# Preparing the first attention group of an adaptive-norm block: q and k written straight into the scores' rows, the preparation in source order, and maxima by half sequences

## The chip, the cores and the metric

The kernel runs on one core of a Trainium2 chip. The metric is the device time of one execution in microseconds; the time before is the median of three executions. Engines are named as in the profile: PE is TensorE's matrix products, PEld its weight loads, DVE is VectorE, ACT is ScalarE, POOL is GpSimd, SP is SyncE, whose queue issues most of the DMAs.

## What is computed

A transformer block with adaptive layer norms on x of shape (4, 1024, 256), in float32, 16 heads of 16. Shapes below are those of one of the 4 batches where nothing else is said.

```python
mod = (silu(c) @ wmod).reshape(4, 6, 1, 256)
sa, ca, ga, sb, cb, gb = six parts of mod          # ga, gb: at least 0.25 in size
h = layernorm(x) * (1 + ca) + sa
q, k, v = split(h @ qkv_w.T)                       # 16 heads of 16
att = softmax(q @ k.T / 4) @ v
x = x + ga * (att @ proj_w.T + proj_b)
h = layernorm(x) * (1 + cb) + sb
loss[n] = mean((relu(h @ W_enc[n] + b_enc[n]) @ W_dec[n] + b_dec[n] - h) ** 2)   # 8 experts
n = connected_idx[argmin(loss)]
x = x + gb * (h @ W_base + b_base + relu(h @ W_down[n] + b_down[n]) @ W_up[n] + b_up[n])
```

## The kernel before

**Scores twice.** Four heads make a group; there are 4 batches x 4 groups = 16 groups. For each, the kernel needs the maximum of every row of scores ahead of the softmax. So it makes the scores twice. First untransposed: `row_max` (L409) makes `ps` = q by k for 128 queries, 512 keys and two heads at a time (L448), and VectorE reduces it (L455). One such tile is a pair, and a group has 32. Then transposed: `step_of`'s `begin` (L534) makes `pt` = k by q, adds the rows' maxima `mt` by a second product with the constant `pick` (L542), and ScalarE takes the exponential `es` (L550). `weigh` (L502) multiplies `es` by v with a column of ones beside each column, `vaug` (L506). A group has 16 steps (2 halves of 512 queries by 8 tiles of 128 keys), each with two `pt` tiles; 256 steps in all.

**Rows of the scores.** To be exact enough in the fast 32-bit mode, q and k are each split in a rounded part and the rest. A row of 16 dimensions becomes 64 rows: q rounded, q rounded, q rest, q rest against k rounded, k rest, k rounded, k rest. `qk_chunk` (L326) makes q or k of eight heads (128 rows by 512 columns) and splits it into `qhl`/`khl`; `expand` (L393) then writes each of the four parts by its own DMA of 32 rows to every fourth partition of `q64`/`k64` (L402).

**Maxima to rows.** When a set of pairs is done, `to_row` (L414) turns the maxima by a PE transpose `pmx` (L416), copies and splits them (DVE, POOL) and sends them by `mdram` to DRAM and back to `mt` (L423, L431). The argument `apart` makes this happen once for each half of the queries; otherwise once for the group. Only the first group has it.

**Order.** PE's instructions are in source order by hand (`manual_schedule`, L82). The other engines' order is decided by a scheduler from the source order and the dependences. The preparation (L896 to L988) makes the condition `cs` (L140) from `c`, turns the weights (`turn_weights`, L153), makes the modulation (`modulation`, L160), normalises the first batch (`norm_items`, L252, through `norm_first`, L301), makes q and k of the first eight heads and spreads two groups of them, fills constants (`mt`, `pick`, `vaug`), and starts the remaining loads (`load_rest`, L199). Then 16 pairs of the first group run, and after each of them one item of the list `beside` (L959): weight turns for v, the products for v (L370), the second modulation, the gate rows (L182), the turns for proj, the biases. Then come the first maxima's `to_row`, four pairs more, and the main loop.

**Pace of the maxima.** In the main loop, `wanted(k)` (L984) says how many pairs shall be given by step k. Before: 20 at step 0, 32 at step 4, 64 at step 12, and from then each group is complete five steps ahead of its first step. Dense work beside (q and k of later heads, v, projections, the experts) is spread over the steps by streams of items.

**Buffers.** Three PSUM tiles of two banks (`big`) serve `ps`, `pt` and the experts' `pr`; two single banks (`acc`, `msc`) serve the rest and, through `spare_tile`, the preparation. `xin` has three buffers for x of later batches; `fu` (L351) has one.

Of the kernel before, what the change touches and what calls it, by code (L numbers as in the profile page):

```python
# [8 lines left out]
F32 = mybir.dt.float32  # L9
# [8 lines left out]
P = 128  # L18
# [8 lines left out]
def tile_adaln_block(  # L27
# [54 lines left out]
    ctx.enter_context(tc.manual_schedule(engines={mybir.EngineType.PE}))  # L82
# [13 lines left out]
    qn = stage.tile([P, 3 * NC, D], F32, name="qn")  # L96
    qkv_rows = qkv_w.rearrange("(o p) i -> p o i", p=P)
    nc.scalar.dma_start(qn[:, : 2 * NC, :], qkv_rows[:, : 2 * NC, :])
    wm = stage.tile([P, NC, 6 * D], F32, name="wm")
    wmod_rows = wmod.rearrange("(c p) e -> p c e", p=P)  # L100
    nc.sync.dma_start(wm[:, :, : 2 * D], wmod_rows[:, :, : 2 * D])
    for u in range(NT // 4, NT // 2):
        x_in[0, u] = load_two(0, u)
    nc.scalar.dma_start(qn[:, 2 * NC :, :], qkv_rows[:, 2 * NC :, :])
    nc.scalar.dma_start(wm[:, :, 2 * D :], wmod_rows[:, :, 2 * D :])
    pn = stage.tile([P, NC, D], F32, name="pn")
    nc.scalar.dma_start(pn, proj_w.rearrange("(o p) i -> p o i", p=P))
# [5 lines left out]
    nc.gpsimd.memset(neghalf, -0.5)  # L113

# [38 lines left out]
    def turn_weights(dst, src, o, tile):  # L153

        pt = tile([P, NC, P], f"pw_{dst.name}_{o}")
        for c in range(NC):
            nc.tensor.transpose(pt[:, c, :], src[:, o, c * P : (c + 1) * P], ident)
        nc.scalar.copy(dst[:, :, o * P : (o + 1) * P], pt)

    def modulation(first, tile):  # L160
# [13 lines left out]
        nc.vector.tensor_copy(modc[:, first], pm[:, 0])  # L174
        nc.vector.tensor_scalar_add(modc[:, first + 1], pm[:, 1], 1.0)
# [125 lines left out]
    def norm_first(b, between=()):  # L301
# [3 lines left out]
        items = [("X", alloc)]  # L305
        for half in range(NH):
            items += norm_items(
                lambda t, half=half: x_in[b, (half * TH + t) // 2][:, t % 2, :],
                lambda: hT_of[b],
                SA,  # L310
                CA,
                b,
                half,
                f"n1_{b}_{half}",
                b == 0,
            )
            if half == 0:
                items += between
        return items
# [6 lines left out]
    def qk_chunk(b, ch):  # L326
        def part(n, which, h, c, s={}):
# [17 lines left out]
            if c == NC - 1:  # L345
                hl = split[key]
                if alone:
                    nc.scalar.copy(hl[:, 0, hs], pq)
                    nc.vector.tensor_tensor(hl[:, 1, hs], pq, hl[:, 0, hs].bitcast(F32), ALU.subtract)
                    return  # L350
# [42 lines left out]
    def expand(b, g, i):  # L393

        ch, r0 = g // GC, (g % GC) * HG * HD
        for which, order in (("q", (0, 0, 1, 1)), ("k", (0, 1, 0, 1))):
            hl = split[which, b, ch]
            t = wa.tile([P, S], F32R, tag=f"{which}64{i}", name=f"{which}64_{b}_{g}_{i}", bufs=3)
            r = slice(r0 + 2 * i * HD, r0 + (2 * i + 2) * HD)
            for n, part in sorted(enumerate(order), key=lambda x: x[1]):  # L400
                queue = nc.scalar if alone and which == "k" and g == 0 else nc.sync
                queue.dma_start(t[n::4, :].bitcast(F32), hl[r, part, :].bitcast(F32))  # L402
            duos[which, b, g, i] = t

# [4 lines left out]
    def row_max(b, g, apart=False):  # L409
# [30 lines left out]
        for halves in [[hq] for hq in range(NH)] if apart else [list(range(NH))]:  # L440
            pairs = [(i, hq, t, h) for i in range(2) for hq in halves for t in range(TH) for h in range(NH)]
            for i, hq, t, h in pairs:
# [452 lines left out]

    cs = condition()  # L896
    for o in range(2 * NC):
        turn_weights(wqkv, qn, o, big_tile)
    modulation(SA, big_tile)
    all_of(Stream(norm_first(0)))  # L900
    all_of(Stream(qk_chunk(0, 0)))
    for g in range(2):
        for i in range(2):
            expand(0, g, i)
    mean_w = cst.tile([P, P], F32, name="mean_w")
    nc.gpsimd.memset(mean_w, 1.0 / (S * D))
    iota_i = cst.tile([P, NE], I32, name="iota_i")
    nc.gpsimd.iota(iota_i, pattern=[[1, NE]], base=0, channel_multiplier=0)
    iota_e = cst.tile([P, NE], F32, name="iota_e")
    nc.vector.tensor_copy(iota_e, iota_i)  # L910
    part_i = cst.tile([P, 1], I32, name="part_i")
    nc.gpsimd.iota(part_i, pattern=[[0, 1]], base=0, channel_multiplier=1)
    part_f = cst.tile([P, 1], F32, name="part_f")
    nc.vector.tensor_copy(part_f, part_i)

    mt = []
    for n in range(2):
        t = cst.tile([P, S], F32R, name=f"mt{n}")  # L920
        nc.gpsimd.memset(t.bitcast(F32), 0.0)
        mt.append(t)
    picks = []
    for i in range(2):
        t = cst.tile([P, 1], F32, name=f"row{i}")
        nc.vector.tensor_tensor(t, ident[:, i : i + 1], ident[:, 2 + i : 3 + i], ALU.add)
        for r in (DUO + i, DUO + 2 + i):
            nc.vector.tensor_tensor(t, t, ident[:, r : r + 1], ALU.add)
        pick = cst.tile([P, P], F32R, name=f"pick{i}")
        nc.vector.tensor_copy(pick, t.to_broadcast([P, P]))  # L930
        picks.append(pick)

    NV = NG + 1
    vaug = []
    for n in range(NV):
        t = cst.tile([P, NT, HG, STRIP], F32, name=f"vaug{n}")
        nc.gpsimd.memset(t, 1.0)
        vaug.append(t)
    mpad = []
    for n in range(2):  # L940
        t = cst.tile([P, P], F32, name=f"mpad{n}")
        nc.gpsimd.memset(t, 0.0)
        mpad.append(t)

# [12 lines left out]


    beside = [lambda o=o: turn_weights(wqkv, qn, o, spare_tile) for o in range(2 * NC, 3 * NC)]  # L959
    beside += [lambda item=item: [f() for f in item[2]] for item in v_all(0)]  # L960
    beside += [lambda: modulation(SB, spare_tile), lambda: gate_rows(spare_tile)]
# [244 lines left out]
```

## Time and profile before

| | us |
|---|---|
| median of 3 executions | 1191.78 (1190.69 to 1195.03) |
| the profiled execution | 1194.91, its span 1193.1 |
| first pair of scores (`ps`) | at 42.47 |
| transpose of the first maxima (`pmx`) | at 72.24 |
| first exponential (`es`) | at 80.00 |
| one maximum of a pair, DVE | 1.22 |
| one exponential, ACT | 1.02 |

The mean granted clock of TensorE is 0.978 of full. Times in the profile are microseconds from the start of the span unless marked ns. A group of instructions is told by its line, its engine and `out<-in` by the program's names, then how many there were. Of each wait, the profile names the engine or DMA that ended it. The time at which an engine is idle costs nothing unless the engine bounds the time. The granted clock (PEclk) is a share of the full TensorE clock. A product in full 32-bit shows as two records, one in the fast mode as one.

### The profile page before, as it was taken

To read this page: it belongs to the slowest core of one execution; us is meant where nothing else is said; L and a number is where in the kernel's file an instruction comes from. 1 tells how busy PE (TensorE), PEld (TensorE's weight loads), DVE (VectorE), ACT (ScalarE), POOL (GpSimd) and SP (SyncE) were. 2 spreads that over 40 slices of the span, in tenths; PEclk is the share of its full clock that TensorE was granted. 3 is DMA by queue.
4 is the path that set the end of the run, shared out by engine and by line. 5 is a ranking of instruction groups with operands and counts; after the bars stand their busy time and mean duration, and the time that the engine had idled before them with its cause. 6 is when DMAs were issued, how large, how long until landed. Compare 5 with 4: busy or idle time off the path is not lost.

```text
span 1193.1 us, 16436 instructions
## 1 busy us (share of the span) xinstructions
PE 1077.8 (90%) x6324; PEld 476.5 (40%) x6324; DVE 791.9 (66%) x975; ACT 692.3 (58%) x928; POOL 254.8 (21%) x271
## 2 busy tenths in 40 slices
PE   4768889999999889999999889999999889899995
PEld 3423333434444333345444333345444333344443
DVE  4477977777687666767678666676778777701264
ACT  2114466665666677654556667654655676647662
POOL 3155000200314002240224201140222200042003
PEclk9869999999999999999999999999999999999998
DMA  6522130122121201113131200204040300011001
GB/s 203 142 81 55 41 77 18 50 69 54 44 60 36 61 15 48 54 43 82 38 110 27 56 15 24 64 27 103 17 131 8 76 1 18 15 58 53 18 1 47
DMA packets 42582, 63.92 MB, mean 54 GB/s; under 512 B 13052, under 2 KB 28436, under 8 KB 42504
## 3 DMA queue, kind: packets, MB, share of 16 engines
q1 hardware_dynamic: 40000, 58.41, 18.2%
q10 hardware_dynamic: 1736, 3.15, 0.8%
q0 software_dynamic: 768, 1.31, 0.5%
q8 instruction: 50, 0.82, 0.3%
q14 instruction: 28, 0.23, 0.1%
HBM read 19.39 MB, written 5.19 MB: 21 GB/s over the span
## 4 chain that ended last, share of the span: by engine, by line
PE 69%; ACT 11%; DVE 10%; DMA 4%; issue 4%; POOL 2%; SPq 0%; ACTq 0%; DVEq 0%; POOLq 0%
PE pt L542 18%; PE pv L506 18%; PE ps L448 10%; ACT es L550 6%; DVE mx L455 5%; PE ph L626 4%; PE pr L647 3%; PE pq L338 3%; PE pvp L370 3%; ACT df L655 3%; DVE df L650 3%; PE ppj L591 2%; PE pf L761 2%; PE pk L338 2%; PE ptn_n L284 2%
## 5 line engine op out<-in xcount | busy, mean ns | idle before, releaser
L455 DVE TENSOR_REDUCE mx<-ps 128x2 f32<-128x1024 f32 x512 | 611.8, 1220 | 191.9 <-PE ps L448 188.2
L550 ACT ACTIVATE es<-pt 128x1024 f32<-128x1024 f32 x512 | 510.8, 1022 | 296.2 <-PE pt L542 289.5
L506 PE MATMUL pv<-es,vaug 128*32 128x512 f32 x2048 | 274.6, 607 | 0.1
L448 PE MATMUL ps<-k,q 64*128 64x512 f32 x1024 | 236.4, 461 | 35.0 <-ACT es L550 10.4
L542 PE MATMUL pt<-q,k 64*128 64x512 f32 x1024 | 239.0, 451 | 21.8 <-ACT es L550 10.7
L542 PE MATMUL pt<-mt,pick 64*128 64x512 f32 x1024 | 209.4, 393 | 4.6 <-DMA mt<-mdram 4.6
L448 PEld LDWEIGHTS ps<-k,q 64*128 64x128 f32 x1024 | 98.3, 186 | 201.4 <-issue 92.5
L542 PEld LDWEIGHTS pt<-q,k 64*128 64x128 f32 x1024 | 99.3, 184 | 170.7 <-DVE mx L455 96.8
L655 ACT ACTIVATE df<-df,fbias 128x512 f32<-128x512 f32 x128 | 91.1, 713 | 55.0 <-DVE df L650 55.0
L542 PEld LDWEIGHTS pt<-mt,pick 64*128 64x128 f32 x1024 | 100.4, 186 | 15.6 <-DMA mt<-mdram 5.8
L650 DVE TENSOR_TENSOR df<-pr,h2T 128x1024 f32<-128x1024 f32 x64 | 77.4, 1222 | 42.5 <-PE pr L647 20.7
L506 PEld LDWEIGHTS pv<-es,vaug 128*32 128x32 f32 x2048 | 40.5, 108 | 100.1 <-issue 90.8
L647 PE MATMUL pr<-he,wdec 64*128 64x512 f32 x256 | 64.3, 614 | 6.3 <-ACT es L550 6.2
L484 POOL TENSOR_TENSOR aT<-aT,su 128x512 f32<-128x512 f32 x14 | 17.8, 1273 | 238.9 <-DMA su<-rdram 189.5
L626 PE MATMUL ph<-h2T,wenc 128*128 128x512 f32 x128 | 63.6, 623 | 0.0
L781 DVE TENSOR_TENSOR x<-pf,x 128x512 f32<-128x512 f32 x16 | 10.8, 687 | 54.3 <-PE pf L772 22.1
L353 POOL CAST qhl<-fu_q 128x512 fp32r<-128x512 f32 x14 | 8.5, 610 | 178.4 <-ACT fu_q L352 175.9
L267 POOL TENSOR_TENSOR rstd_n<-ve_n,neghalf 128x4 f32<-128x4 f32 x16 | 16.8, 1048 | 102.2 <-DVE ve_n L265 96.4
L761 PE MATMUL pf<-wbg,h2T 128*128 128x256 f32 x128 | 37.4, 425 | 0.0
L647 PEld LDWEIGHTS pr<-he,wdec 64*128 64x128 f32 x256 | 21.6, 185 | 37.3 <-ACT es L550 13.2
L284 PE MATMUL ptn_n<-ident,xh_n 128*128 128x128 f32 x128 | 23.2, 311 | 14.0 <-ACT h2T L285 6.6
L626 PEld LDWEIGHTS ph<-h2T,wenc 128*128 128x128 f32 x128 | 22.3, 192 | 33.0 <-issue 31.8
(134 smaller groups left out, 755.8 us busy)
## 6 DMA issues: line engine op xcount, KB each, us to landing
q<-qhl SPq DMA_DIRECT2D x128, 128.0 KB
k<-khl SPq DMA_DIRECT2D x120, 128.0 KB
xin<-in_L_attn_x_dram SPq DMA_DIRECT2D x16, 256.0 KB
x<-in_L_attn_x_dram SPq DMA_DIRECT2D x8, 512.0 KB
aT<-ou SPq DMA_DIRECT2D x32, 128.0 KB
out_dram<-x SPq DMA_DIRECT2D x16, 256.0 KB
su<-rdram SPq DMA_DIRECT2D x14, 256.0 KB
wm<-in_L_wmod_dram ACTq DMA_DIRECT2D x1, 1024.0 KB
```

The costliest lines, as they stand in the source:

```text
L284: nc.tensor.transpose(pt[:, t, :], s["xh"][:, t, c * P : (c + 1) * P], ident)
L338: nc.tensor.matmul(pq, wqkv[:, c, n * D + ch * P : n * D + (ch + 1) * P], hT[:, c, hs], start=(c == 0), stop=(c == NC - 1),)
L448: nc.tensor.matmul(ps[:, a, :], q[r, t0 : t0 + P], k[r, h * HALF : (h + 1) * HALF], start=True, stop=True,)
L455: nc.vector.tensor_reduce(mx[:, h, hq, i::2, t], ps, AX.X, ALU.max, negate=True)
L506: nc.tensor.matmul(acc[h][j * STRIP : (j + 1) * STRIP, :], va[:, kt, j, :], es[j // 2][:, j % 2, :], start=(kt == 0), stop=(kt == NT - 1),)
L542: nc.tensor.matmul(pt[:, a, :], k[r, kt * P : (kt + 1) * P] if first else picks[i][r, :], q[r, hs] if first else mt[n % 2][r, hs], start=f ...
L550: nc.scalar.activation(e, pt, AF.Exp, scale=SCALE)
L626: nc.tensor.matmul(s["ph"], wenc[:, c, 2 * pr : 2 * pr + 2, :].rearrange("p n h -> p (n h)"), s["h2T"][:, c, hs], start=(c == 0), stop=(c ...
L647: nc.tensor.matmul(two[:, i, :], wdec[r, pr, c * P : (c + 1) * P], he[r, :], start=True, stop=True)
L650: nc.vector.tensor_tensor(df, two, h2T[:, c, hs].unsqueeze(1).to_broadcast([P, 2, HALF]), ALU.subtract)
L655: nc.scalar.activation(df[:, i, :], df[:, i, :], AF.Square, bias=bdec_of(e, c), accum_out=s["acc"][:, e, c, h : h + 1],)
L761: nc.tensor.matmul(po[u][:, t, :], s["h2T"][:, c, t0 : t0 + P], s["wbg"][:, c, :], start=(c == 0), stop=False,)
```

## The change

1. **Order.** From the start of the preparation until the main loop, ACT, DVE, POOL and SP also keep the source order; the source is rearranged for it. The constants, zeros and ones come first, then the statistics of the first half of x, `cs`, the normalised first half, the weights, the second half's statistics, the modulation. Of `vaug` only the columns of ones are filled, not all. A tile `warm` and three products of it (`keep_on`) are added.
2. **Loads.** x of the first batch is first in SP's queue, the q and k weights and the first part of `wmod` in ACT's; the v weights, the rest of `wmod` and the proj weights follow in SP's. The v weights lie in a buffer of `xin`.
3. **First group.** For its heads, q and k are not spread by DMA. `turn_weights` also writes the turned weights with every column four times (`wide`, in two `xin` buffers). A product with `wide` then gives 128 rows, each dimension four times, for two heads (`widened`): ScalarE rounds it into `fu`, and VectorE writes `fu` times `less` plus the product, where `less` is -1 in the rows that hold a rest and 0 in the others. There are four such products for the first half of the sequence, ahead of the first scores, and two more (k's second half) beside them. q's second half comes by DMA from the ordinary split (`second_half`).
4. **Beside.** The four q and k products of the first eight heads, which came before the scores, are now items of `beside`, and their split goes over GpSimd as it does later in the kernel. The turns of the remaining q and k weights come at its end.
5. **expand** uses two DMAs of 64 rows for q and two for k in place of four and four of 32 rows; all on SP.
6. **Maxima.** In all four groups of the first batch the maxima go to `mt` by halves of the queries, and the order of pairs within a half is keys' half, head pair, tile. `wanted` now asks 20 at step 0, 32 at step 3, then runs evenly to 160 at step 59, the first batch's end; later batches as before.
7. The modulation's two results are copied by ScalarE, not VectorE.

```diff
-    ctx.enter_context(tc.manual_schedule(engines={mybir.EngineType.PE}))
+    ctx.enter_context(tc.manual_schedule(engines={ET.PE}))
+    begin_order = ctx.enter_context(ExitStack())
+    begin_order.enter_context(tc.manual_schedule(engines={ET.Activation, ET.DVE, ET.Pool, ET.SP}))
...
-    nc.sync.dma_start(wm[:, :, : 2 * D], wmod_rows[:, :, : 2 * D])
+    nc.scalar.dma_start(wm[:, :, : 2 * D], wmod_rows[:, :, : 2 * D])
...
+    vn = xin.tile([P, NC, D], F32, tag="xin", name="vn")
+    wide = {w: xin.tile([P, NC, D], F32, tag="xin", name=f"wide_{w}") for w in "qk"}
+    nc.sync.dma_start(vn, qkv_rows[:, 2 * NC :, :])
+    nc.sync.dma_start(wm[:, :, 2 * D :], wmod_rows[:, :, 2 * D :])
...
-        nc.gpsimd.memset(t, 1.0)
+        nc.gpsimd.memset(t[:, :, :, 1::2], 1.0)
...
+        if wide is not None:
+            for c in range(NC):
+                nc.scalar.copy(
+                    wide[:, c, :].rearrange("p (j n) -> p j n", n=4),
+                    pt[:, c, : HG * HD].unsqueeze(2).to_broadcast([P, HG * HD, 4]),
+                )
...
-                if alone:
-                    nc.scalar.copy(hl[:, 0, hs], pq)
-                    nc.vector.tensor_tensor(hl[:, 1, hs], pq, hl[:, 0, hs].bitcast(F32), ALU.subtract)
-                    return
...
-            for n, part in sorted(enumerate(order), key=lambda x: x[1]):
-                queue = nc.scalar if alone and which == "k" and g == 0 else nc.sync
-                queue.dma_start(t[n::4, :].bitcast(F32), hl[r, part, :].bitcast(F32))
+            for n in range(2):
+                rows = hl[:, n : n + 1, :].to_broadcast([2 * HD, 2, S]) if which == "k" else hl
+                nc.sync.dma_start(t[n::2].bitcast(F32), rows)
...
+    def widened(which, i, h):
+        hs = slice(h * HALF, (h + 1) * HALF)
+        key = (which, 0, 0, i)
+        if key not in duos:
+            duos[key] = wa.tile([P, S], F32R, tag=f"{which}64{i}", name=f"{which}64_0_0_{i}", bufs=3)
+        pq = spare_tile([P, HALF], f"pw{which}_{i}_{h}")
+        for c in range(NC):
+            nc.tensor.matmul(
+                pq,
+                wide[which][:, c, i * P : (i + 1) * P],
+                hT_of[0][:, c, hs],
+                start=(c == 0),
+                stop=(c == NC - 1),
+            )
+        fu = wa.tile([P, HALF], F32, tag="fu", name=f"fu_{which}_{i}_{h}", bufs=1)
+        nc.scalar.copy(fu.bitcast(F32R), pq)
+        nc.vector.scalar_tensor_tensor(duos[key][:, hs], fu, less[which], pq, ALU.mult, ALU.add)
+
+    def second_half(i):
+        hl = split["q", 0, 0][2 * i * HD : (2 * i + 2) * HD, :, HALF:].bitcast(F32)
+        for n in range(2):
+            nc.sync.dma_start(duos["q", 0, 0, i][n::2, HALF:].bitcast(F32), hl)
...
+            if apart:
+                pairs = [(i, hq, t, h) for hq in halves for h in range(NH) for i in range(2) for t in range(TH)]
...
+    first, second = [Stream(items) for items in norm_first(0)]
+    all_of(first, most=TH + 1)
     cs = condition()
-    for o in range(2 * NC):
-        turn_weights(wqkv, qn, o, big_tile)
+    keep_on(1)
+    keep_on(2)
+    all_of(first, most=TH)
+    for o, w in ((0, "q"), (NC, "k")):
+        turn_weights(wqkv, qn, o, big_tile, wide=wide[w])
+    all_of(second, most=TH + 1)
     modulation(SA, big_tile)
...
+    widened("k", 0, 0)
+    widened("q", 0, 0)
+    widened("k", 1, 0)
+    all_of(second)
+    widened("q", 1, 0)
...
+    beside = [lambda i=i: widened("k", i, 1) for i in range(2)]
+    beside += [lambda item=item: [f() for f in item[2]] for item in qk_chunk(0, 0) if item[0] == "D"]
...
-            yield from row_max(b, g)
+            yield from row_max(b, g, apart=b == 0)
...
-        ends = [(0, FIRST + 4), (4, PAIRS), (STEPS - 4, 2 * PAIRS)] + [
-            (first_step[bg] - LEAD, PAIRS * (n + 3)) for n, bg in enumerate(groups[2:])
+        ends = [(0, FIRST + 4), (3, PAIRS)] + [
+            (first_step[bg] - LEAD, PAIRS * (n + 1)) for n, bg in enumerate(groups) if bg[0]
         ]
```

## What was predicted

> **What bounds the kernel now.** I read the totals first, then the engines by stretches of 20 us, then the chain of waits for the first 140 us, because everything in the diff but one line lies ahead of the main loop.
>
> From part 1 of the page:
>
> ```profile
> PE 1077.8 (90%) x6324; PEld 476.5 (40%) x6324; DVE 791.9 (66%) x975; ACT 692.3 (58%) x928; POOL 254.8 (21%) x271
> ```
>
> TensorE is the bound of the whole: 115.3 us of the 1193.1 us span are all that it idles. So a change here can pay only by idle time of TensorE or by time at a low clock. Where these lie is told by the stretches (start:end, length, PE busy, PEld, DVE, ACT, POOL, then granted clock, DMA share, GB/s):
>
> ```profile
> 0.00:20.00 20.00, 2.65 (x11) 1.69 (x11) 9.83 (x33) 2.95 (x6) 8.61 (x18) 1.00 0.89 272
> 20.00:40.00 20.00, 14.53 (x48) 9.35 (x48) 6.91 (x29) 5.45 (x8) 9.04 (x15) 0.95 0.41 97
> 40.00:60.00 20.00, 17.53 (x71) 11.21 (x72) 9.77 (x10) 3.88 (x18) 0.00 (x0) 0.76 0.53 144
> 60.00:80.00 20.00, 11.80 (x43) 5.27 (x42) 16.14 (x24) 1.49 (x4) 8.48 (x8) 0.67 0.27 81
> 80.00:100.00 20.00, 16.49 (x78) 6.04 (x74) 13.53 (x16) 8.19 (x9) 19.62 (x18) 0.77 0.19 57
> 100.00:120.00 20.00, 17.65 (x101) 7.03 (x101) 16.77 (x18) 8.93 (x10) 4.94 (x7) 1.00 0.26 65
> 120.00:140.00 20.00, 16.14 (x92) 6.54 (x92) 18.29 (x17) 9.30 (x10) 1.88 (x2) 1.00 0.23 59
> 220.00:240.00 20.00, 20.00 (x120) 8.47 (x120) 13.38 (x12) 11.89 (x14) 5.22 (x6) 1.00 0.25 66
> ```
>
> The first four rows hold 46.5 us of PE work in 80 us: 33.5 us idle, and the clock falls to 0.67. The next three idle 9.7 us more. From 140 to 220 us PE works 73.28 of 80 us, from 220 to 340 us 117.79 of 120: there is little left to win. The first exponential starts at 80.0 us, and that is the point from which I measure the two halves of the sum. The chain of waits up to there (start, length, what):
>
> ```profile
> 9.74 10.19 issue
> 19.92 3.55 PE pm L167 x16
> 27.28 3.87 PE pq L338 x8
> 38.46 4.00 DMA q<-qhl
> 42.47 0.80 PE ps L448 x2
> 62.68 9.15 DVE mx L455 x8
> 72.24 0.45 PE pmx L416
> 83.28 2.50 DMA xin<-in_L_attn_x_dram
> ```
>
> Three holes are seen: PE waits 10.2 us for the condition `cs` (VectorE makes it only at 19.7 us, behind work whose `xin` landed late), 7.9 us for the spreading DMAs of q and k, and from 62.7 us on it runs at the pace of VectorE's maxima (8 in 9.15 us, with the clock at 0.5 to 0.7).
>
> **The change, part by part.**
>
> *Front to the first score.* The order of the built program is now fixed for all engines. VectorE has 12 small operations on `ident`, then `iota_e`, which waits for GpSimd. GpSimd first fills two `mt` (0.94 and 1.04 us) and five `vaug`, 1.02 us each at 1024 elements (5.12 us for five). They now write 512 elements at a stride of two. No row shows a strided fill: 0.5 us each if it goes by elements, 1.0 if by the span; I take 0.5, since 128 elements cost 0.2 and 1024 1.02. So `iota_e` at about 6.3 us (8.9 at the other end). VectorE's small operations took 0.8 to 1.1 us where they lay beside those fills, so I add 1 us. Then the first half's statistics, as in the row from 3.69 to 5.84 us: 2.1; and three operations for `cs`, 0.5: `cs` at about 10 us, not 19.8. The weights `wm` are 512 KB in the second queue behind `qn`; at the 272 GB/s of the first row, the 2 MB of x, q/k weights and `wm` are there by 8 to 10 us. pm: 3.55 us as at 19.9, or 1.95 as at 56.4; I take 3, and with modc end at 13.5. The first half's transposes and their two activations (23.47 to 26.09 us before): 2.6, to 16.1. Then in PE's order three widened products (four records of 0.48, so 1.93 each by the row of pq), two transpose groups (1.9), the fourth product: 4 x 1.93 + 1.9 = 9.6, and 0.8 for handing tiles to ScalarE and VectorE and back. **First score at about 26.5 us, not 42.5**; 24.5 to 30 with the ends above. Two warm-up products before the weights and the extra copies of `wide` on ScalarE (4 x 0.4) lie in the wait for `cs`; were that gone they would cost 3 us.
>
> At this place a rule speaks against the sum. The Trainium skill (TensorE: Matmul & The Clock Gate, Parts 1 and 4) says that full clock needs some 3.4 us of sustained activity and that transposes do not count as busy. By it, pm and eight transposes leave the array cold, and the first two products cost 3.9 instead of 1.93 each: 30.4 us. But the row of before has just pm and sixteen transposes from 19.92 to 27.28, and then pq at 3.85 for 8 records, full speed. I go by the row.
>
> *The stage of the first maxima.* It holds more PE work than before, for two widened products and the four of the ordinary q and k have come into it. Sixteen pairs of scores x 0.5 = 8; six products x 1.93 = 11.6; v's two weight turns 1.0; gate rows 2.5 (3.2 at the low clock before); four v products x 1.95 = 7.8; pm 1.9; the proj and remaining q/k turns and biases, 2.4: 35.2. To this 1.8 for waits: the single buffer `fu` now goes through GpSimd (cast 0.61 + difference 1.27), which also makes four normalised tiles of the next batch (1.21 each) in between; that holds ScalarE in order, hence v's weight copies. 26.5 + 37 = 63.5 for the transpose of the maxima, not 72.2. VectorE's sixteen maxima (19.6) no longer trail: they are hidden under 37 us of PE work. From that transpose to the first exponential it took 7.8 us (72.24 to 80.0), four steps of which stay as they are: **first exponential at about 71.5, 8.5 us earlier**. Bounds 67.5 and 78.
>
> *The main loop, to step 59.* Before, `wanted` asks 4 pairs a step up to step 12, then 2.1 and 2. Now it asks 4 a step for three steps and 128 pairs over 56 steps, 2.3 a step. The first 60 us after 80 hold 40 maxima and 23 exponentials, 5.2 us a step; from 140 to 220 us 52 and 47, 3.4 us a step. The pairs are not removed: TensorE gets each one's 0.45 us later. So the worth is idle and cold time. Idle 9.7 in 60 us (16%) should come to the 8.4% of the next 80 us, whose load of maxima, 2.2 a step, is nearest: 4.6 gained. Low clock from 80 to 100 (0.77): 3 gained, if PE enters warm; it again has some 5 us of idle before the first exponential, so 2. Against it: three more max transposes, 1 us. And VectorE's queue: after the fourth maximum of the second half come the statistics of the next batches' x. Of these the one that reads `xin_1` waits for a load that waits for GpSimd to have centred the tiles before it, and GpSimd now has the gated projection weights (1.29), the gated bias (0.73) and two additions (1.23 each) ahead of that. Queued behind the waiting statistics are two maxima, and behind them both score tiles and so TensorE. Before, VectorE idled 1.8 us here; I get 4.5 (load at 81.0, maxima done at 76.5): minus 2.7, between 0 and -7. Loop: +2.9, between -4 and +10.
>
> *Rest.* q and k spread by half as many DMAs of twice the bytes, on SP only: the 0.6 us that each issue takes is halved. In their new order, SP's loads of the next x wait for PE's last use of `wide` (27 and 32 us), behind them lie the second halves of q (39, when GpSimd has split it), group 1's rows (49) and the gate rows (56); the first of these is asked for at 64, group 1 at 80. GpSimd waits for `conn_i` behind 5 MB of loads, 20 us at 272 GB/s, and has nothing due before 34. So all of it has slack; in the whole loop PE waited 4.6 us for `mt` and for spread q or k only once, at 42 us. I take 0; were the slack gone, a late spread would cost its 4 us once per group. From batch 1 the plan is as before: 0.
>
> Sum: 1194.9 (span 1193.1 and 1.8 around it) - 8.5 - 2.9 = 1183.5. That execution stands 3.1 above the median of 1191.8, so against the median I say **1180.4**.
>
> **The rivals.**
> *A, as summed* (0.50): 1174 to 1185.
> *B, the loop takes it back* (0.20): the pairs put off return in steps 12 to 59, where PE idles only 6.7 us from 140 to 220, and VectorE's stall is at its long end. For it: TensorE is the bound, and 2.3 pairs a step are more than what the 140-to-220 stretch carries. Against: 9.7 us of idle just before. 1191.8 - 8.5 + 4 = 1187.
> *C, both halves at their good ends* (0.17): first exponential at 67.5 and +7 in the loop: 1191.8 - 12.5 - 7 = 1172, or a few less.
> *D, slower by a low clock* (0.13): between 12 and 63.5 us PE has 50 us of work at full clock, with eight widened products (15.4 us) that it did not have. The clock was 0.76 and 0.67 from 40 to 80 us of before. At 0.85 throughout, 9 us are lost and the 8.5 are gone; at 0.7, 21: 1191.8 - 11.4 + 21 = 1201. Against: those low stretches had PE waiting; between 50 and 58 us, dense, it shows 1.00.
>
> **The numbers.** Differences below 0.5%, 6 us, are about what a measurement of this kernel cannot tell from none. Faster by more (below 1185.8): nearly all of A, C, a third of B: 0.70. Within: 0.18. Slower (over 1197.8): most of D: 0.12. The range, 1167 to 1193, leaves out D and C's far end; A's own is 1174 to 1185.
>
> **What would show it.** In the changed profile: first score near 26.5, max transpose near 63.5, first exponential near 71.5 us; no wait of scores for q's spreading; the clock at 0.9 or more from 20 to 60 us; about 32 maxima in the first 11 steps; VectorE idle near 77 to 81 us on `xin`; from step 59 the same pace as now. It is wrong if `cs` comes after 14 us, if the clock from 15 to 60 us is under 0.85, or if PE idles over 16 us in the 140 us after the first exponential.

## The result, and the profile after

The changed kernel takes 1199.31 us (median of 6 executions, 1198.30 to 1200.87), the kernel before, run beside it, 1193.4 (1189.54 to 1199.05, 6 executions): a ratio of 1.0046, 95% interval 1.0026 to 1.0067. Predicted were 1180.4 us, with 1167 to 1193 as the range. The change costs about 6 us where 11 us of gain were expected. The profiled execution took 1198.3 us with a span of 1196.5; before it was 1194.91 and 1193.1.

Part 1 of the page of the changed kernel, as before:

```profile
PE 1094.1 (91%) x6357; PEld 482.2 (40%) x6357; DVE 797.7 (67%) x980; ACT 697.3 (58%) x942; POOL 261.6 (22%) x285
```

TensorE idles 102.4 us of the span instead of 115.3, and is still slower: it has 16.3 us more busy time, with only 33 more records. Part of that is work at half clock. The stretches (columns as before: start:end, length, PE, PEld, DVE, ACT, POOL, granted clock, DMA share, GB/s):

```profile
0.00:20.00 20.00, 16.44 (x45) 8.98 (x46) 14.15 (x44) 5.66 (x14) 7.63 (x21) 0.83 0.87 264
20.00:40.00 20.00, 18.98 (x56) 7.40 (x54) 14.01 (x21) 6.08 (x10) 7.00 (x13) 1.00 0.12 31
40.00:60.00 20.00, 17.80 (x87) 11.38 (x85) 11.11 (x10) 6.54 (x27) 15.04 (x12) 0.97 0.74 166
60.00:80.00 20.00, 11.19 (x39) 4.83 (x41) 11.93 (x23) 3.23 (x5) 13.25 (x13) 0.50 0.33 95
80.00:100.00 20.00, 18.34 (x93) 7.44 (x97) 15.05 (x19) 8.23 (x9) 10.18 (x12) 0.85 0.09 27
220.00:240.00 20.00, 18.93 (x127) 7.49 (x123) 15.08 (x14) 12.79 (x15) 4.49 (x6) 1.00 0.31 69
```

The first 60 us are what they were meant to be: from 20 to 60 us TensorE is busy for 36.8 of 40 us, at a granted clock of 0.98. The hole is now one, from 60 to 80 us: 11.19 us of work at a clock of 0.50. The chain of waits up to there (start, length, what):

```profile
10.06 2.84 PE pm L227 x16
14.79 3.39 PE pwk L472 x4
18.18 1.72 PE pwq L472 x4
25.46 0.65 PE ps L534 x3
75.42 2.67 DMA xin<-in_L_attn_x_dram
```

PE no longer waits for spread rows of q, and the first exponential starts at 68.25 us instead of 80.00. So where did that lead go? Each step's first exponential (`es`, L636, before L550) was read off both traces. This is how much earlier (minus) or later it stands than before, with four of the experiments told of below:

| step | before at, us | changed | e1 | e2 | e6 | e13 |
|---|---|---|---|---|---|---|
| 0 | 80.0 | -11.8 | -10.5 | +1.5 | -10.4 | -14.0 |
| 4 | 103.3 | -6.0 | -3.8 | +1.0 | -4.0 | -16.2 |
| 12 | 143.9 | -17.6 | -15.4 | +1.0 | -15.6 | -26.7 |
| 60 | 309.2 | -6.9 | -4.7 | +1.0 | -4.8 | -14.7 |
| 128 | 598.7 | -6.7 | -4.7 | +2.6 | -4.7 | -15.0 |
| 144 | 657.9 | -1.0 | -5.4 | +7.7 | -5.4 | -15.4 |
| 192 | 874.0 | -0.1 | -5.5 | +8.6 | -5.5 | -14.2 |
| 208 | 934.2 | +4.4 | -6.3 | +14.5 | -6.4 | -15.2 |
| 255 | 1123.8 | +4.1 | -6.5 | +12.7 | -3.1 | -13.3 |

Four things are in the column "changed". The front gains 11.8. The first four steps give 5.8 of it back. Steps 4 to 12 gain another 11.6, and steps 12 to 60 take 10.7 back. And in three short stretches, at about 602, 683 and 885 us, 11 us are lost for good (5.7, 0.9 and 4.5), in batches whose plan was said to be as before.

VectorE at the loop's start shows the first loss (the timeline; in brackets the idle time before the instruction and what ended it):

```profile
78.12 0.43 DVE L320 BATCH_NORM_STATS2 bs_n<-xin 128x6 f32<-128x256 f32 x1 [7.02 <-DMA xin<-in_L_attn_x_dram]
78.46 2.34 DVE L541 TENSOR_REDUCE mx<-ps 128x2 f32<-128x1024 f32 x2
```

The statistics are those of batch 2's x (counted from 0), put by the scheduler some 60 steps ahead of their place in the source. The two maxima behind them wait too, and with them both score tiles.

The second kind of loss is at 602 us. First SP's queue of the changed kernel, the time of each issue, then VectorE:

```profile
596.79 0.57 SPq L461 DMA_DIRECT2D k<-khl  x1
597.46 0.53 SPq L605 DMA_DIRECT2D aT<-ou  x1
598.04 1.25 SPq L615 DMA_DIRECT2D sdram<-ou  x1
599.38 0.60 SPq L461 DMA_DIRECT2D k<-khl  x1
600.03 0.59 SPq L461 DMA_DIRECT2D q<-qhl  x1
600.98 0.77 SPq L554 DMA_DIRECT2D rs<-sdram  x1
```

```profile
597.99 1.23 DVE L541 TENSOR_REDUCE mx<-ps 128x2 f32<-128x1024 f32 x1 [0.21 <-PE ps L534]
604.59 0.35 DVE L557 RECIPROCAL rs<-rs 128x32 f32<-128x32 f32 x1 [5.38 <-DMA rs<-sdram]
604.86 2.29 DVE L541 TENSOR_REDUCE mx<-ps 128x2 f32<-128x1024 f32 x2
```

`sdram` takes the softmax sums out to DRAM (8 KB), `rs` brings them back as 128x32 (16 KB), and VectorE's reciprocal stands in its queue among the maxima. It waits 5.38 us. Before, the same place looks like this, with two spreads of k of 128 KB between the first two lines:

```profile
601.72 0.56 SPq L529 DMA_DIRECT2D sdram<-ou  x1
605.20 0.53 SPq L468 DMA_DIRECT2D rs<-sdram  x1
607.36 0.35 DVE L471 RECIPROCAL rs<-rs 128x32 f32<-128x32 f32 x1 [1.33 <-DMA rs<-sdram]
```

The wait was 1.33 us. Over the whole kernel, VectorE's idle time in front of the 14 reciprocals is 17.0 us in seven waits, before 5.3 in six. TensorE, which gets no score tile while VectorE stands, also falls to half clock for 6.8 us from 604.8.

### The profile page after: what moved, and what is told of

It is laid out like the page before. It is cut to its first block, busy times and chain, and to the rows that moved or that the text cites. A ratio compares the mean times of both kernels' runs of the same rounds, so it can differ in the third digit from the quotient of the medians.

```text
span 1196.5 us, 16380 instructions
## 1 busy us (share of the span) xinstructions
PE 1094.1 (91%) x6357; PEld 482.2 (40%) x6357; DVE 797.7 (67%) x980; ACT 697.3 (58%) x942; POOL 261.6 (22%) x285
## 4 chain that ended last, share of the span: by engine, by line
PE 70%; ACT 11%; DVE 8%; DMA 4%; issue 4%; POOL 2%; SPq 0%; DVEq 0%; ACTq 0%; POOLq 0%
PE pt L628 18%; PE pv L592 18%; PE ps L534 10%; ACT es L636 6%; PE ph L712 4%; PE pr L733 3%; PE pq L400 3%; ACT df L741 3%; PE pvp L428 3%; DVE df L736 2%; PE ppj L677 2%; DVE mx L541 2%; PE pk L400 2%; PE pf L847 2%; PE ptn_n L344 1%
## 5 line engine op out<-in xcount | busy, mean ns | idle before, releaser
L636 ACT ACTIVATE es<-pt 128x1024 f32<-128x1024 f32 x512 | 510.9, 1022 | 308.3 <-PE pt L628 299.5
L534 PEld LDWEIGHTS ps<-k,q 64*128 64x128 f32 x1024 | 99.1, 188 | 192.8 <-issue 76.5
L628 PEld LDWEIGHTS pt<-mt,pick 64*128 64x128 f32 x1024 | 101.7, 188 | 15.6 <-DMA mt<-mdram 6.2
L504 POOL CAST mrow<-mfull 32x128 fp32r<-32x128 f32 x20 | 5.6, 281 | 199.2 <-DVE mfull L502 199.2
L867 DVE TENSOR_TENSOR x<-pf,x 128x512 f32<-128x512 f32 x16 | 10.8, 687 | 54.2 <-PE pf L858 22.1
L327 POOL TENSOR_TENSOR rstd_n<-ve_n,neghalf 128x4 f32<-128x4 f32 x16 | 16.6, 1034 | 88.4 <-DVE ve_n L325 84.6
L344 PE MATMUL ptn_n<-ident,xh_n 128*128 128x128 f32 x128 | 21.9, 296 | 15.2 <-ACT h2T L345 6.5
```

Source lines behind the costliest of these rows:

```text
L534: nc.tensor.matmul(ps[:, a, :], q[r, t0 : t0 + P], k[r, h * HALF : (h + 1) * HALF], start=True, stop=True,)
L628: nc.tensor.matmul(pt[:, a, :], k[r, kt * P : (kt + 1) * P] if first else picks[i][r, :], q[r, hs] if first else mt[n % 2][r, hs], start=f ...
L636: nc.scalar.activation(e, pt, AF.Exp, scale=SCALE)
```

## The experiments

Theory S: the two bigger spreading DMAs make `rs` late, and VectorE's reciprocal passes that on. Its first rival, L: TensorE is the bound, the loop takes any lead back, and the places are accidental. Each time of before was measured beside the kernel that it stands with.

**e1: four spreads in the loop.** `expand` of before for the main loop, that of the change in the preparation.

```diff
+            if not alone:
+                for n, part in sorted(enumerate(order), key=lambda x: x[1]):
+                    nc.sync.dma_start(t[n::4, :].bitcast(F32), hl[r, part, :].bitcast(F32))
```

> The changed kernel, but q and k of the main loop are again spread by four DMAs of 32 rows each instead of two of 64; the preparation keeps its two. Theory S (the small load of the sums, rs, comes late behind the bigger spreading DMAs in SP's queue, VectorE's reciprocal waits 5.4 us for it in order, and TensorE waits for the maxima behind that): the lead of 6.9 us that the changed kernel still has at step 128 is kept to the end, the waits for rs at about 602 and 885 us fall to about 1.5 us, time about 1188 (11 less than the changed kernel's 1199, 5 less than before). Rival L (TensorE bounds the loop and takes the lead back in any case, the three losses of 5.7, 1.0 and 4.5 us only happen to stand at those places): the losses reappear at other places and the time is 1197 or more.

Measured: 1187.39 us, before 1193.37; ratio 0.9954 (0.9941 to 0.9966). The lead of 4.7 us at step 128 is kept to the end. At the same place SP and VectorE show:

```profile
596.98 0.56 SPq L620 DMA_DIRECT2D sdram<-ou  x1
598.69 1.13 SPq L466 DMA_DIRECT2D k<-khl  x2
599.92 0.54 SPq L559 DMA_DIRECT2D rs<-sdram  x1
```

```profile
602.05 0.35 DVE L562 RECIPROCAL rs<-rs 128x32 f32<-128x32 f32 x1 [0.91 <-DMA rs<-sdram]
```

This kernel stands 2.0 us later at this place. Allowing for that, `sdram` is issued 3.1 us earlier than in the changed kernel, and `rs` lands 2.1 us after its issue instead of 3.6. The first spread of k, on which SP stood until GpSimd had cast `khl` at 596.76, now comes behind `sdram`, not ahead of it. VectorE's order is the same: the reciprocal follows the 286th maximum in both.

**e2: only the two spreads.** The other direction: before, with two DMAs of 64 rows in the loop.

```diff
+            if not alone:
+                for n in range(2):
+                    rows = hl[r].bitcast(F32)
+                    if which == "k":
+                        rows = rows[:, n : n + 1, :].to_broadcast([2 * HD, 2, S])
+                    nc.sync.dma_start(t[n::2].bitcast(F32), rows)
```

> The kernel before, with only this part of the change: q and k of the main loop are spread by two DMAs of 64 rows each. Theory S: SP's queue then has the same order as in the changed kernel (sums out, two DMAs of 256 KB, rs, two more), VectorE waits some 5.4 us for rs at two or three places, and the time is some 11 us above before, about 1204. Rival L: half as many issues of twice the bytes make no difference, within 2 us of before.

Measured: 1205.75 us, ratio 1.0108 (1.0079 to 1.0137). This part alone costs 12 us, and the waits for `rs` sum to 19.0 us. S holds both ways so far as the spreads go, and L falls: e1 kept the whole lead that it had at step 128. What passes the lateness on is left to e6.

**e3: the old pace of maxima**, `apart` for the first group alone.

```diff
-            yield from row_max(b, g, apart=b == 0)
+            yield from row_max(b, g)
...
-        ends = [(0, FIRST + 4), (3, PAIRS)] + [
-            (first_step[bg] - LEAD, PAIRS * (n + 1)) for n, bg in enumerate(groups) if bg[0]
+        ends = [(0, FIRST + 4), (4, PAIRS), (STEPS - 4, 2 * PAIRS)] + [
+            (first_step[bg] - LEAD, PAIRS * (n + 3)) for n, bg in enumerate(groups[2:])
```

> The changed kernel with the pace of maxima of before (64 pairs at step 12, each group complete five steps ahead) and the maxima by halves only for the first group. Theory P (the pairs put off are a loan: from step 12 to 59 they are paid back one for one): the lead over before at step 12 is only about 8 us, not 17.6, at step 60 it is 7 as in the changed kernel, and the time is within 3 us of the changed kernel's. Rival (the even pace itself costs TensorE idle time, since VectorE is then asked for 2.3 maxima in each step of 12 to 59): the lead at step 60 stays near 11 us and the time falls by 4 or more.

Measured: 1199.82 us, ratio 1.0052 (1.0037 to 1.0068), as the changed kernel. The lead is 6.7 us at step 12 and 6.7 at step 60. So the even pace is a loan: 11 us lent by step 12, all paid back by step 60, and worth nothing.

**e4: source order kept for eight steps more**, on ACT, DVE, POOL and SP.

```diff
-    begin_order.close()
...
     for k0 in range(0, len(order) * NT, 2):
+        if k0 == 8:
+            begin_order.close()
```

> The changed kernel, but the source order of ACT, DVE, POOL and SP is kept for eight steps more, into the main loop, so that the statistics of a later batch's x can't be put ahead of the loop's maxima in VectorE's queue. If VectorE's wait of 7.0 us for xin at 71 to 78 us is real loss: it is gone, the first exponential is some 4 us earlier, the lead at step 12 is larger, and the time is about 5 us less, 1194. If it lies beside the wait for the maxima's way through DRAM to mt anyway: the first exponential stays at 68 and the time within 2 us of the changed kernel's.

Measured: 1204.88 us, ratio 1.0096 (1.0070 to 1.0122): a miss. The wait of 7.0 us is gone, and the lead at step 8 is 19.7 us instead of 11.8. But the statistics only come later, and wait for `xin` there: 2.6 us at 97.5, 5.5 at 116.6, 3.5 at 139.4 us. At step 60 the lead is 0.6. The wait is a real loss, and it moves with the statistics.

**e5: `rs` issued by GpSimd**, in the changed kernel.

```diff
-        nc.sync.dma_start(rs, sdram[n].rearrange("j (a c) -> (j a) c", c=few[0]))
+        nc.gpsimd.dma_start(rs, sdram[n].rearrange("j (a c) -> (j a) c", c=few[0]))
```

> The changed kernel with its two big spreading DMAs, but the one small load rs (16 KB, 14 of them) is issued by GpSimd's queue instead of SP's; nothing else is moved by it but one maximum past one reciprocal. Theory S (the loss of 12 us is the lateness of rs in SP's queue, passed on by VectorE's in-order reciprocal): VectorE's idle time in front of the reciprocals falls from 17.0 us to 5 or less, the waits at about 602 and 885 us go, and the time is about 1188. Rival T (the bigger transfers cost the same time on other ways: they hold the DMA engines, or the other small transfers of SP's queue come late too): 1195 or more.

Measured: 1206.35 us, ratio 1.0097 (1.0073 to 1.0120): worse than the changed kernel, and a miss for S, which had 1188. VectorE's waits before reciprocals rise to 28.3 us. At the place of 602 us `sdram` is still issued behind a spread of k and held for 1.22 us. GpSimd stands idle in front of nine of its 14 issues of `rs` until `sdram<-ou` has landed, 135 us in all, and what it has to do next stands behind. So moving the second DMA alone leaves the first one late; how much GpSimd's own queue adds was not traced.

**e6: the reciprocal on GpSimd**, both DMAs left where they were; `one32` is a constant tile of -1.

```diff
-            nc.vector.reciprocal(rs, rs)
+            nc.gpsimd.tensor_tensor(rs, rs, one32, ALU.pow)
```

> The changed kernel with its two big spreading DMAs; the reciprocal of rs (128x32) is taken by GpSimd as a power of -1 instead of by VectorE. rs is as late as before in SP's queue, but VectorE's queue no longer holds an instruction that waits for it. Theory S (the price is paid because VectorE's maxima stand behind the waiting reciprocal): the time falls to about 1187. Rival U (the late spread of q and k or the late su itself is what TensorE waits for): 1197 or more. GpSimd's rstd of 128x4 took 1.04 us, so 32 elements may take up to 8 us each, 14 times, on an engine that is 22% busy: if that delays the split of q and k, 2 to 4 us are lost of this.

Measured: 1190.01 us, before 1195.36; ratio 0.9957 (0.9943 to 0.9970). The group of the reciprocal:

```profile
L559 POOL TENSOR_TENSOR rs<-rs,one x14: 5425/5434/5467, 177.4 to 1028.0; 128x32 f32<-128x32 f32 x14
```

It takes 5.43 us instead of 0.35, the bigger DMAs are still there, and yet at every step of the table up to 208 this kernel has e1's lead within 0.2 us. So the price of the two spreads is what VectorE's queue holds up behind the reciprocal; up to there neither the spread rows nor `su` (the reciprocals on their way back) are what TensorE waits for. Of the lead, 3.3 us go at steps 230 to 232, where e1 loses nothing, and this is the slower reciprocal's own price. TensorE waits 3.05 us here:

```profile
1042.71 1.08 PE L826 MATMUL pmid<-h2T,wd 128*64 128x512 f32 x4 [3.05 <-DMA wd<-in_L_ffn_W_down_dram,rd0u]
```

GpSimd issues the load of `wd` behind its product with `su`, which comes later by the longer reciprocal. e11 and e13 show the same wait (3.3 and 3.0 us), e1 has none.

**e7: no warming products**, in e1's kernel.

```diff
-    keep_on(0)
...
-    keep_on(1)
-    keep_on(2)
```

> The first experiment's kernel (the changed one with four spreads in the loop) without the tile's three warming products (keep_on). In the changed kernel the clock falls to half at 10.8 us all the same, for 6.8 us. If these products do nothing for the clock that counts: first score at 25.4 within 0.5 us, time 1187 within 1.5. If they keep the array warm for pm: pm takes 3.5 us or more and the first score comes up to 3 us later, of which the end would see most: about 1190.

Measured: 1190.5 us, before 1195.36; ratio 0.9971 (0.9955 to 0.9987), e1's being 0.9954. TensorE's timeline in the front:

```profile
10.03 3.55 PE L226 MATMUL pm<-cs,wm 128*128 128x4 f32 x16 [1.28 <-ACT wide_k L213]
13.44 1.95 PE L343 MATMUL ptn_n<-ident,xh_n 128*128 128x128 f32 x8
15.47 3.78 PE L476 MATMUL pwk<-hT,wide_k 128*128 128x512 f32 x4
19.04 2.32 PE L476 MATMUL pwq<-hT,wide_q 128*128 128x512 f32 x4
```

The first product runs at half rate after 5.4 us of `pm` and transposes; the second (1.88 us at full rate) has the first of its four records at half rate. The trace's clock record begins with full clock at 19.91 us, during the second one. The first score comes at 26.84 us, in e1's kernel at 25.38. In all kernels with the warming products it comes at 25.5 us or sooner. So the products are worth 1.5 us at that point.

**e8: VectorE in source order through the whole loop**, in e1's kernel.

```diff
     begin_order.close()
+    ctx.enter_context(tc.manual_schedule(engines={ET.DVE}))
```

> The first experiment's kernel, with VectorE kept in source order through the whole main loop. The statistics of a later batch's x can then not be put ahead of the loop's maxima, and each reciprocal stands where the source puts it. If the waits of VectorE for small or late loads are what the schedule loses: the 7.0 us wait for xin at 71 to 78 us and the 3.1 us for rs go, the first four steps give nothing back, and the time is about 1187 - 6 = 1181. If source order makes VectorE wait elsewhere (for instance statistics right behind their load, as in the fourth experiment, which lost 9.0 us in two such waits between 110 and 140 us): 1190 or more.

Measured: 1217.49 us, ratio 1.0191 (1.0167 to 1.0216). To step 64 it gains 9.5 us over e1, then loses 36 in the later batches; why it loses there was not worked out. The second expectation held in the end and the first one for the first batch alone, which led to e10.

**e9: `sdram` issued by ScalarE**, in the changed kernel.

```diff
-                nc.sync.dma_start(sdram[ch * NH + h][j0 : j0 + HG, :], ou[1::STRIP, :])
+                nc.scalar.dma_start(sdram[ch * NH + h][j0 : j0 + HG, :], ou[1::STRIP, :])
```

> The changed kernel with its two big spreading DMAs; only the small DMA sdram<-ou (8 KB, 28 of them) is issued by ScalarE, right behind the copy that makes ou, instead of by SP. In the changed kernel's trace at 590 to 605 us SP stands 6.4 us on a k<-khl that waits for GpSimd's cast of khl, and sdram<-ou, whose data ScalarE had ready at 594.5, is issued behind it at 598.0 and again held 1.25; rs lands at 604.6. Theory Q (the two-DMA form matters by where it puts sdram in SP's queue, ahead of which the first k<-khl now stands, and not by its bytes): VectorE's idle time before the reciprocals falls from 17.0 us to 9 or less and the time to 1194 or less; rs itself still stands in SP's queue, so not all of the 12 us comes back. Rival B (bytes: the 256 KB transfers hold the DMA engines, so that any small transfer lands late): the idle time stays above 14 us and the time at 1198 or more. Each of the 28 issues takes some 0.55 us of ScalarE, which is 58% busy; no more than 1 us of loss from that.

Measured: 1197.38 us, before 1194.40; ratio 1.0026 (1.0016 to 1.0035). The idle time is 16.6 us: a miss for Q. `sdram` is issued at 594.60, 3.4 us earlier, but in SP's queue:

```profile
600.58 1.21 SPq L554 DMA_DIRECT2D rs<-sdram  x1
```

`rs` still stands behind two spreads of k and one of q, and lands 3.7 us after its issue. With the first DMA on time, the second is as late as ever.

**e10: VectorE in source order to step 60**, in e1's kernel.

```diff
     begin_order.close()
+    begin_order.enter_context(tc.manual_schedule(engines={ET.DVE}))
...
     for k0 in range(0, len(order) * NT, 2):
+        if k0 == 60:
+            begin_order.close()
```

> The first experiment's kernel (four spreads in the loop) with VectorE kept in source order through the first batch's 60 steps, and free after that. In the eighth experiment source order gained 9.5 us by step 64 and lost 36 after it. The statistics of batch 1's x stand at 48 and 70 maxima, where they were at 5 and 20; those of batch 2 are put at 72 to 77, where their load may be late as in the fourth experiment. If the start's wait for xin is a real loss: the lead at step 4 is 9 to 12 us more, some 4 us is lost again at about step 20, and the time is 1187 - 5 = 1182. If the wait only moves to the later statistics in full: 1187 or more.

Measured: 1187.79 us, before 1194.40; ratio 0.9950 (0.9931 to 0.9968), the same as e1. The lead at step 20 is 26.6 us against e1's 15.6; 12.1 us are lost again between steps 20 and 32 (2.3 in e1, the loan), where batch 2's statistics now stand, and the waits for `rs` are 7.1 us. The second expectation held.

**e11: e10 with the reciprocal on GpSimd.** The diff is that of e6.

> The tenth experiment's kernel with the reciprocal of rs on GpSimd as in the sixth. VectorE still idles 3.1 us before reciprocals in the first experiment's kernel; if all of it comes back, 1 to 3 us below the tenth's time; if GpSimd's 5.43 us for each reciprocal delays the centring of x or the split of q and k, equal or up to 3 us slower.

Measured: 1184.14 us, before 1194.40; ratio 0.9914 (0.9894 to 0.9934). 3.6 us below e10, a little more than expected.

**e12: both small DMAs out of SP's queue**, the diffs of e5 and e9 together.

> The changed kernel with its two big spreading DMAs, and both small transfers of the chain out of SP's queue: sdram<-ou is issued by ScalarE as in the ninth experiment, rs<-sdram by GpSimd as in the fifth. Each alone left the other late (VectorE's idle time before the reciprocals 16.6 and 28.3 us, against 17.0). Theory Q (the place in SP's queue, twice): with sdram issued at 594.6 and landed by about 597, GpSimd can issue rs as soon as its casts of khl end, near 598.2, it lands near 600.5 and the reciprocal waits 1 us or less; in sum 8 us of idle time or less, and 1191 or less. Rival B (the bytes: a small transfer lands late behind 256 KB transfers, whichever queue issues it): rs takes 3.5 us or more from issue to landing beside the spreads, 12 us or more of idle time, 1195 or more. Rival G (GpSimd's own queue holds rs up behind the centring of x and the splits): the wait is at other places, 1193 or more.

Measured: 1198.87 us, before 1191.33; ratio 1.0055 (1.0036 to 1.0075): no gain. The trace is of an execution of 1193.43, 5 us under the median, so only its single waits are used. At the place of 602 us:

```profile
599.62 0.60 POOL L554 DMA_DIRECT2D rs<-sdram  x1
```

```profile
603.79 0.35 DVE L557 RECIPROCAL rs<-rs 128x32 f32<-128x32 f32 x1 [3.06 <-DMA rs<-sdram]
```

The wait is 3.06 us instead of 5.38, so here the place in SP's queue was part of it. But `rs` lands 4.2 us after its issue, where the median of the 14 is 2.0: this is rival B. At 468 and 749 us, behind GpSimd's own queue, the waits are 4.05 and 4.30 instead of 2.31 and 2.59, as rival G had it, and the sum is 19.1 us. So Q misses all its numbers (1 us, 8 us, 1191), and all three of B's are met (landing over 3.5 us, idle time over 12, 1195 or more).

**e13: e11 with source order to step 68.**

> The eleventh experiment's kernel with VectorE's source order kept to step 68 instead of 60. That leaves the statistics of batch 2's first x at 175 to 179 maxima, where their load is long done, instead of 72 to 77, where the eleventh lost 4.5 us between steps 20 and 32. If that loss is VectorE's wait for that load: the 4.5 us stay, and the time is about 1180. If it only moves to steps 64 to 72 (the eighth experiment lost 1.9 there): 1182 to 1184.

Measured: 1183.33 us, before 1191.33; ratio 0.9926 (0.9903 to 0.9949). The profiled execution took 1180.2 us. The lead at step 60 is 14.7 us against e11's 10.2, as the first expectation has it, but the two ratios' intervals overlap. The stretches after the first exponential:

```profile
60.00:80.00 20.00, 15.07 (x68) 6.34 (x66) 15.63 (x14) 6.39 (x7) 8.83 (x8) 0.72 0.20 64
80.00:100.00 20.00, 18.66 (x119) 7.78 (x115) 13.85 (x14) 10.63 (x12) 4.51 (x6) 1.00 0.23 55
```

Against 11.19 us at 0.50 and 18.34 at 0.85 in the changed kernel: without the wait for `xin`, the hole at 60 to 80 us is half filled and the clock is full from 80 us on. This kernel differs from the changed one in three things (four spreads, the reciprocal, VectorE's order), so the comparison shows the hole filled by them together; e10 and e11 have much the same lead at step 4 (15.9 and 14.9 us). e11 and e13 are faster than both kernels of the case.

## Why the prediction was wrong

**The front: right, and 3 us too careful.** `cs` was made at 9.82 us (10 predicted), `pm` took 2.84 (3), the first score came at 25.39 (26.5), the transpose of the maxima at 60.09 (63.5), the first exponential at 68.25 (71.5). The gain is 11.8 instead of 8.5. The clock from 20 to 60 us is 0.98 in place of rival D's 0.7 to 0.85.

**The rule I set aside, and the row I went by.** I took full rate for the products after `pm` and transposes from one row of before, where 7.4 us of such work came ahead. The Trainium skill (TensorE: Matmul & The Clock Gate, Part 4) says that a transpose does not count as busy in the same way. In e7, with 5.4 us of `pm` and transposes and no warming products, the first product took 3.78 us, nearly the 3.9 that I had worked out by the rule, and the second 2.32: 2.2 us over full rate for the two, where the rule gave 3.9 and my row nothing. But before does not bear the rule out: its trace grants full clock from 27.63 us, when nothing but `pm`, transposes and the first 0.35 us of the products had run since 19.92. And my row was one draw. e2 has the same preparation; there full clock came at 28.89 us, and the same eight records took 4.75 us, not 3.85. Which of this work counts stays open. For taking the warming products away, e7's expectation was up to 3 us; it was 1.5. With them, in the changed kernel, the first product still took 3.39 us, the granted clock being at half from 10.8 to 17.7 us. That cost 1.5 us, and it was luck that an estimate 2.6 us too long elsewhere hid it.

**The loop to step 59: wrong in its sign, -4.9 for +2.9.** The stall on `xin_1` was found in its place with its cause and its followers. Its size was off, 7.0 us for 4.5: the load was issued at 75.42 and the statistics began at 78.12, but VectorE had no work from 71.1 on, not from 76.5, since the stage ahead of it came earlier. And what is queued behind it was priced by the wait alone: TensorE also stayed at half clock until 85.9 us, 0.56 over the first 20 us after the first exponential, where I had counted on a warm entry worth 2 us. The 4.6 us for less idle time did not come: PE idles 9.4 us in those 60 us, before 9.7. The spread of the maxima was priced as a gain; e3 shows it at nothing. This is rival B's mechanism: the pairs put off come back in steps 12 to 59, one for one.

**The rest: this is the step that failed most.** "In their new order ... So all of it has slack ... I take 0" and "From batch 1 the plan is as before: 0". It measured 11.0 us in the trace (from -6.9 at step 60 to +4.1 at step 255), and 12 by e1 and e2. I looked at the spread rows, asked whether they would be late, and rightly found slack. I did not ask what else stands in SP's queue. `expand` runs in every batch, so its DMAs are moved past `sdram` and `rs` there, and the one instruction that waits for `rs` is in order on VectorE. Of the seven waits only the two longest show in the steps: those of 5.4 and 5.5 us cost 5.7 and 4.5 us; the two of 2.3 and 2.6 us cost 0.3 at most. The 0.9 us at 683 us are no such wait: no reciprocal stands there, but the clock is at half for 3.4 us, and e13, without these waits, loses 1.1 us at the same steps.

**Two slips.** Rival D counts eight widened products; there are six, four ahead of the scores and two beside them. And before, `wanted` asked three pairs a step for the first four steps, not four. Neither moves the forecast by much.

**The sum by what was measured**: 1194.9 - 11.8 + 4.9 + 11.0 = 1199.0; the profiled execution took 1198.3.

**What is left open.** Why the two bigger DMAs make `rs` late has two parts, and the runs show both without dividing them cleanly. One is the place: the built order has the first spread of k ahead of `sdram`, and spreads ahead of `rs`. The other is the landing, 3.6 to 4.2 us beside the 256 KB transfers against 2.1 beside those of 128 KB. For the second, the traces show a backlog at this place. In the changed kernel SP issues 896 KB between 596.8 and 600.6 us (k twice, `aT`, q), some 240 GB/s, and in e1 640 KB between 596.4 and 601.7 us, some 125 GB/s; from 597 to 605 us the DMA engines move 136 and 133 GB/s. The packets of `rs` (128 of 128 bytes) begin 2.4 us after its issue in the changed kernel and 1.2 us after it in e1. In the 2 us after its issue the DMA engines are busy for a share of 0.99 in the changed kernel and 0.65 in e1 (last column but one):

```profile
601.00:603.00 2.00, 0.69 (x8) 0.00 (x0) 0.00 (x0) 0.59 (x1) 0.00 (x0) 1.00 0.99 162
600.00:602.00 2.00, 2.00 (x18) 0.71 (x18) 1.13 (x1) 1.26 (x2) 0.02 (x1) 1.00 0.65 143
```

So in the changed kernel more is issued than is moved, and the small transfer comes after it. That the bytes alone would do this is not shown: a kernel with the same order and half the bytes wasn't tried.

## What to carry to other kernels

When DMAs become fewer and bigger, list every small transfer that shares their queue, in every stage that uses the helper, and the in-order instruction that waits for it: halving the issues cost 1% through a 16 KB load. An instruction that waits for a small round trip should not stand in the queue of the engine whose results the bound engine needs; on an engine with time to spare it took fifteen times as long, and the time still fell by some 10 us. Work put off is a loan where the bound engine is busy later, and waits moved ahead by a scheduler move again when one pins them.

## What the runs showed of the hardware

- In each trace the granted clock changes only at multiples of 3.41 us from its first change (stretches of 3.41, 6.83, 10.24 us), and these points lie elsewhere in every trace. In the twelve kernels with the warming products, full clock comes back between 15.9 and 18.4 us.
- The profile prints a clock of 1.00 for the time ahead of the trace's first clock record. In e7 this record begins at 19.91 us; before it, a product takes 3.78 us that takes 1.88 later. There the durations tell the rate, and the printed 1.00 does not.
- Issuing a DMA can hold SP: `sdram` takes 0.53 to 0.69 us before, and up to 1.86 us beside the bigger spreads; `rs` up to 0.53 before, 1.80 after.
- GpSimd's power of 128x32 takes 5.43 us, of 128x4 1.04; VectorE's reciprocal of 128x32 takes 0.35.
- A small VectorE operation beside GpSimd's fills can take many times its time: in the changed kernel one `pick` (128x128) took 3.72 us from 1.91 us on, until the fills of `mt` and `vaug` ended at 5.56; the next one took 0.23.
